# A four-layer vision-mamba stack on one core: the first and the last image's row work moved beside the scans, another order of the scan directions, and empty steps in the side work

## The chip, the cores and the metric

The kernel runs on one NeuronCore of a Trainium2 chip. The metric is the device time of one launch in microseconds. Five engines take part, each with its own instruction queue that is worked off in order: TensorE (PE in the profile, its weight loads PEld), VectorE (DVE), ScalarE (ACT), GpSimd (POOL) and SyncE (SP), which issues all DMAs here. An instruction at the head of a queue that waits for another engine holds up everything behind it in that queue.

## What is computed

Four images of 64 x 64 positions with 128 channels go through four layers. Layers 0, 1 and 3 are selective-scan blocks; layer 2 is a gated block without a scan. The core of a scan block, cut from the reference:

```python
xn = _ln(x); xx, z = split(xn @ in_proj)             # 256 channels each
xc = silu(depthwise_conv3x3(xx) + conv_b)
x0 = xc by rows; x1 = xc by columns                  # L = 4096 positions
xs = stack([x0, x1, x0 reversed, x1 reversed])       # four directions
dts, Bs, Cs = split(x_proj @ xs); delta = softplus(dt_w @ dts + dt_b)
h = exp(delta * A) * h + (delta * x) * B             # 16 states a channel, a scan over L
y = sum over states of h * C, plus Ds * xs; summed over the four directions
y = _ln(y) * silu(z);  x = x + out_proj @ y
x = x + fc2 @ gelu(fc1 @ _ln(x))
```

Layer 2 has two layer norms, products of projections and a mean over the whole image; it sits between the scans of layers 1 and 3.

## The kernel before

**Turns.** One turn is the scan of one image in one scan layer. There are 12 turns, listed in `turns` (L652): images 0 and 1 alternate through layers 0, 1, 3, then images 2 and 3. A turn has 4 directions k (0 and 2 by rows forward and back, 1 and 3 by columns) of 8 chunks each of 512 positions, so 32 chunks. A chunk has 8 periods, a period four `tensor_tensor_scan` on DVE (L799), two with their input from PE (`dbp`, L774) and two with theirs from DVE (`dbv`, L913). ACT makes the decays `da` (L783), POOL multiplies by C (`hc`, L811 and L813), PE sums the states into `yp` (L824), and `leave` (L834) adds `yp` into `y_sb`. Directions run in the order 0, 1, 2, 3. At the end of a turn `leave` issues eight DMAs that store `y_sb` to DRAM (L847).

**Side work.** Everything that is not a scan (output norm, gating, projections, MLP, the gated layer, input norm, convolution) is made by `between(e, frm, to, psums)` (L177) as a list `S` of small steps. It works in rows of 512 positions, 8 rows an image: `output_norm`, `project_z`, `convolve` of the row two back, `silu` with its stores of `x_row` and `x_col`, `mixer_out` (`gate` on POOL, then `project` on PE), `mlp`, then `input_norm`, or `finish` for the last layer, or `gate_sums` and `gate_rest` in the gated layer. With `frm=None` it is the first input norm and convolution of an image (`begin`, `input_norm`, `convolve`). `rest(n)` adds n steps that do nothing, so that other queues may catch up; it stands only after a norm's `mean`, after `project` and after the MLP's `down`, and within `silu`.

While image A is scanned, the steps of image B are dealt out between the scan instructions. `other(number)` (L878) is called four times a period, so a turn has 1024 places ("slots"). It issues steps so that they are spread evenly:

```python
gone = at % (8 * per_turn) * 4 + number
while done < len(steps) and done < len(steps) * (gone - 8) / (4 * 8 * per_turn - 76):
```

that is, over 948 slots from slot 8 on. Turns 1, 2, 7 and 8 carry the plain side work between two scan layers, turns 3, 4, 9 and 10 the gated one, turns 5 and 6 a finished image and a new image's start, turn 11 only a finished image, turn 0 only the start of image 1.

**What no scan covers.** The set-up folds the convolution with the projection for the three scan layers (PE, POOL and DVE, L136 to L154). Then `alone(between(0, None, 0, psums), "first_ps")` runs the start of image 0 with no scan beside it, and after the last scan `alone(after(*turns[-1]), "last_ps")` runs the eight rows of image 3's last layer in the same way. In both, two PSUM banks serve the steps; inside the scans one does.

Of the kernel before, what the change touches and what calls it, by code (L numbers as in the profile page):

```python
# [12 lines left out]
F32 = mybir.dt.float32  # L13
AF = mybir.ActivationFunctionType
ALU = mybir.AluOpType
# [48 lines left out]
def vss_stack_kernel(ctx: ExitStack, tc: tile.TileContext, x: bass.AP, weights, out: bass.AP, n_batch=B, layers=(0, 1, 2, 3)):  # L64
# [25 lines left out]
    wt, conv_d = {}, {}  # L90
    with tc.tile_pool(name="setup", bufs=2) as pool, tc.tile_pool(name="setup_ps", bufs=2, space=PSUM) as psum:
        for i in layers:
            if i == 2:
                g = const.tile([P, GATE_N], F32, name="wg")
                nc.sync.dma_start(out=g, in_=weights[i][0])
                v = {name: g[:, a:z] for name, (a, z) in GATE_AT.items()}

                cb = const.tile([P, 2], F32, name="cb")
                nc.vector.tensor_mul(cb, v["b1"], v["wdw"])
                nc.vector.tensor_add(cb, cb, v["bdw"])  # L100
                v["cb"] = cb
                for name, b, scale in (("b2s", "b2", "beta"), ("bf2s", "bf2", "gamma")):
                    v[name] = const.tile([P, 1], F32, name=name)
                    nc.vector.tensor_mul(v[name], v[b], v[scale])
                wt[i] = v
                continue
            t = const.tile([P, small_n + VSS_N - tail_at], F32, name=f"w{i}")
            for a, z in (VSS_AT["conv_w"], VSS_AT["alog"]):
                nc.sync.dma_start(out=t[:, a - conv_at : z - conv_at], in_=weights[i][0][:, a:z])
            nc.sync.dma_start(out=t[:, small_n:], in_=weights[i][0][:, tail_at:])  # L110
            v = {}
            for name, (a, z) in VSS_AT.items():
                if conv_at <= a < conv_at + small_n:
                    v[name] = t[:, a - conv_at : z - conv_at]
                elif a >= tail_at:
                    v[name] = t[:, small_n + a - tail_at : small_n + z - tail_at]

            v["xp"] = v["xp"].rearrange("p (k m c) -> p k m c", k=2, m=2)
            at, end = VSS_AT["xp"]
            xp = weights[i][0][:, at:end].rearrange("p (b k m c) -> p b k m c", b=2, k=2, m=2)  # L120
            for k in range(2):
                for b in range(2):
                    nc.sync.dma_start(out=v["xp"][:, k, :, b * NX : (b + 1) * NX], in_=xp[:, b, k])
            v["conv_w"] = v["conv_w"].rearrange("p (m t) -> p m t", m=2)
            v["dtb"] = v["dtb"].rearrange("p (k m) -> p k m", k=K)
            a = v["alog"]
            nc.scalar.activation(a, a, AF.Exp)
            nc.vector.tensor_scalar_mul(a, a, -1.0)
            v["a"] = a.rearrange("p (k m n) -> p k m n", k=K, m=2)
            dsum = const.tile([P, 2], F32, name=f"dsum{i}")  # L130
            nc.vector.tensor_reduce(dsum, v["ds"].rearrange("p (k m) -> p m k", k=K), AX.X, ALU.add)
            v["dsum"] = dsum
            v["gelu"] = AF.Gelu if i == 0 else AF.Gelu_apprx_tanh
            wt[i] = v

            in_w = pool.tile([P, DI], F32, tag="in_w", name="in_w")  # L136
            nc.sync.dma_start(out=in_w, in_=weights[i][0][:, :DI])
            conv = pool.tile([P, 2, 9, P], F32, tag="conv", name="conv")
            for m in range(2):
                ps = psum.tile([P, 4, P], F32, tag="ps", name="ps_wt")  # L140
                nc.tensor.transpose(ps[:, 0, :], in_w[:, m * P : (m + 1) * P], ident)
                in_t = pool.tile([P, P], F32, tag="in_t", name="in_t")
                nc.vector.tensor_copy(in_t, ps[:, 0, :])
                diag = pool.tile([P, 9, P], F32, tag="taps", name="taps")
                for t in range(9):
                    nc.gpsimd.tensor_scalar(diag[:, t, :], ident, v["conv_w"][:, m, t : t + 1], None, ALU.mult)
                for t in range(0, 9, 4):
                    count = min(4, 9 - t)
                    ps = psum.tile([P, 4, P], F32, tag="ps", name="ps_taps")
                    for j in range(count):  # L150
                        nc.tensor.matmul(ps[:, j, :], in_t, diag[:, t + j, :], start=True, stop=True)
                    nc.vector.tensor_copy(conv[:, m, t : t + count, :], ps[:, :count, :])
            conv_d[i] = keep.tile([P, 2 * 9 * P], F32, name=f"conv_d{i}")
            nc.sync.dma_start(out=conv_d[i], in_=conv.rearrange("p m t e -> p (m t e)"))  # L154

    def cols(c):
        return slice(c * CH, (c + 1) * CH)


    lanes = []  # L160
    for j in range(2):
# [15 lines left out]
    def between(e, frm, to, psums):  # L177
# [58 lines left out]
        def load():  # L236
# [15 lines left out]
            if frm is None:  # L252
                fetch_x(0)
            else:
                fetch(0)
# [789 lines left out]
```

## Time and profile before

| | us |
|---|---|
| median of 3 runs | 23699.06 (23680.56 to 23713.14) |
| the profiled execution, its time | 23731.97 |
| its span | 23730.2 |
| first scan instruction of turn 0 starts at | 356.50 |
| turns 1, 2, 7, 8 (plain side work), each | 1882 to 1891 |
| turns 3, 4, 9, 10 (gated), each | 2034 to 2048 |
| turns 5, 6 | 1874 and 1876 |
| last scan instruction starts at | 23320.42 |

The profile's page gives each engine's busy time. The answer by windows gives it for any stretch: duration, then each engine's busy time with its number of instructions, the granted TensorE clock, the DMA share and GB/s. The timeline lists instructions in order of time, with the idle time before one in square brackets and the instruction that ended it.

### The profile page before, as it was taken

Reading aid. Unit: us, or ns where it says so; the run is one execution under the profiler, and the core shown is the slowest. Engines: PE = TensorE matmul, PEld = TensorE weight load, DVE = VectorE, ACT = ScalarE, POOL = GpSimd, SP = SyncE. Lnnn points to the kernel's source line nnn. Section 1 sums busy time; section 2 is a strip of 40 time slices with the busy share of each in tenths; the row PEclk is TensorE's granted clock in tenths of the full one; section 3 lists DMA queues with packets and bytes.
Section 4 is the critical chain, followed back from the end, with each engine's and each line's share of the span. In section 5 each row is a group of like instructions: output and inputs, shape, how many; then the busy total and the mean of one; then the engine's idle time right before and its main releaser. Section 6 shows DMA issues by size and latency. Waiting matters only on the chain. (4 is left out here: it accounts for less than half of the span.)

```text
span 23730.2 us, 216913 instructions
## 1 busy us (share of the span) xinstructions
PE 20150.3 (85%) x58234; PEld 10650.4 (45%) x58234; DVE 20432.3 (86%) x20210; ACT 18072.9 (76%) x38792; POOL 19294.9 (81%) x8916
## 2 busy tenths in 40 slices
PE   6888888888888888888888888888888888888886
PEld 3444444444444444444444444444444444444442
DVE  4999998888888888899899889898888888889993
ACT  4777777777877777788788777777777778777774
POOL 4998888888878877788888888888887778788883
PEclk8999999999999999999999999999999999999997
DMA  4444434444334434434434444444443443344331
GB/s 98 139 140 142 131 129 138 130 129 138 124 120 125 136 122 127 132 131 139 137 131 138 133 140 130 127 139 131 130 136 120 121 141 122 120 127 142 129 130 62
DMA packets 2435398, 3060.09 MB, mean 129 GB/s; under 512 B 1753600, under 2 KB 1789056, under 8 KB 2235648
## 3 DMA queue, kind: packets, MB, share of 16 engines
q1 hardware_dynamic: 2434176, 3046.22, 40.8%
q8 instruction: 472, 7.73, 0.1%
q14 instruction: 750, 6.14, 0.1%
HBM read 2784.41 MB, written 261.49 MB: 128 GB/s over the span
## 5 line engine op out<-in xcount | busy, mean ns | idle before, releaser
L811 POOL TENSOR_TENSOR hc<-h,cb 128x1024 f32<-128x1024 f32 x6144 | 14420.8, 2361 | 3596.4 <-DVE h L799 2432.8
L783 ACT ACTIVATE da<-delta,w 128x512 f32<-128x512 f32 x12288 | 8161.9, 713 | 1768.8 <-DVE h L799 1744.1
L824 PE MATMUL yp<-hc,ident 128*128 128x512 f32 x18432 | 9051.9, 617 | 521.6 <-POOL hc L813 310.9
L774 PE MATMUL dbp<-diag,duT 128*128 128x256 f32 x24576 | 6260.7, 400 | 1558.0 <-DVE h L799 1505.2
L799 DVE TENSOR_TENSOR_SCAN h<-da,state,dbp 128x512 f32<-128x512 f32 x5376 | 6563.9, 1261 | 988.7 <-PE dbp L774 807.4
L799 DVE TENSOR_TENSOR_SCAN h<-da,state,dbv 128x512 f32<-128x512 f32 x5376 | 6881.0, 1280 | 487.7 <-ACT da L783 24.1
L774 PEld LDWEIGHTS dbp<-diag,duT 128*128 128x128 f32 x24576 | 4764.8, 199 | 4039.9 <-issue 2586.4
L824 PEld LDWEIGHTS yp<-hc,ident 128*128 128x128 f32 x18432 | 3490.0, 197 | 4862.5 <-issue 3647.9
L913 DVE TENSOR_TENSOR dbv<-dup,bb 128x512 f32<-128x512 f32 x6144 | 4229.9, 688 | 339.4 <-ACT dup L791 175.6
L766 ACT ACTIVATE diag<-ident,bt 128x128 f32<-128x128 f32 x12288 | 3947.9, 401 | 0.3
L813 POOL TENSOR_TENSOR hc<-hc 128x1024 f32<-128x1024 f32 x1536 | 3622.2, 2358 | 120.4
L791 ACT COPY dup<-du 128x512 f32<-128x512 f32 x1920 | 1126.3, 587 | 1336.9 <-DVE dbv L913 1309.8
L361 PE MATMUL gap<-halo,cw 128*128 128x512 f32 x3456 | 1703.8, 606 | 3.1 <-ACT wide L368 3.1
L734 POOL TENSOR_TENSOR du<-delta,xs 128x512 f32<-128x512 f32 x768 | 978.7, 1274 | 114.0 <-ACT delta L722 114.0
L799 DVE TENSOR_TENSOR_SCAN h<-da,dbp 128x512 f32<-128x512 f32 x768 | 893.4, 1201 | 163.4 <-PE dbp L774 104.4
L717 PE MATMUL ps_dt<-xd,dt_w 8*128 8x512 f32 x1536 | 894.0, 662 | 150.1 <-ACT delta L720 85.8
L799 DVE TENSOR_TENSOR_SCAN h<-da,dbv 128x512 f32<-128x512 f32 x768 | 937.4, 1221 | 69.2 <-DVE dbv L913 3.3
L807 ACT COPY state<-h 128x2 f32<-128x2 f32 x5376 | 960.7, 179 | 0.0
L361 PEld LDWEIGHTS gap<-halo,cw 128*128 128x128 f32 x3456 | 639.8, 193 | 698.8 <-issue 666.6
L742 ACT COPY duT<-ps_duT 128x512 f32<-128x512 f32 x768 | 440.1, 573 | 285.5 <-PE ps_duT L740 285.1
L443 PE MATMUL gap<-hid,pw 128*128 128x512 f32 x768 | 455.5, 710 | 166.1 <-ACT hid L434 165.1
L720 ACT ACTIVATE delta<-ps_dt,w 128x512 f32<-128x512 f32 x768 | 524.2, 683 | 46.1 <-PE ps_dt L717 41.4
(122 smaller groups left out, 11353.9 us busy)
## 6 DMA issues: line engine op xcount, KB each, us to landing
cb<-xd_d SPq DMA_DIRECT2D x1536, 1024.0 KB
bb<-xd_d SPq DMA_DIRECT2D x1536, 512.0 KB
xs<-x_row_d SPq DMA_DIRECT2D x192, 512.0 KB
xs<-x_col_d SPq DMA_DIRECT2D x192, 512.0 KB
x_col_d<-down SPq DMA_DIRECT2D x192, 256.0 KB
x_row_d<-wide SPq DMA_DIRECT2D x96, 512.0 KB
y_d<-y_sb SPq DMA_DIRECT2D x96, 512.0 KB
y<-y_d SPq DMA_DIRECT2D x96, 512.0 KB
```

Source lines behind the costliest of these rows:

```text
L361: nc.tensor.matmul(z.ps, z.cw[:, m, t, :], z.halo[c][:, dy : dy + RPC, dx : dx + W], start=(t == 0), stop=(t == 8))
L734: nc.gpsimd.tensor_mul(s.du[:, m], s.delta[:, m], s.xs[:, m])
L766: nc.scalar.activation(s.diag[q][:, t, :, j], ident, AF.Copy, scale=s.bt[:, t, CQ * q + j : CQ * q + j + 1])
L774: nc.tensor.matmul(s.db[:, t * P : (t + 1) * P, :], s.duT[:, t, m, :], s.diag[q][:, t], start=True, stop=True)
L783: nc.scalar.activation(da[:, j], s.delta[:, m], AF.Exp, scale=s.v["a"][:, s.k, m, n : n + 1])
L791: nc.scalar.copy(s.dup, s.du[:, m])
L799: nc.vector.tensor_tensor_scan(s.h[i, side][:, j, s.step], da[:, j, s.step], db[:, s.step], init, ALU.mult, ALU.add)
L807: nc.scalar.copy(s.state[:, m, n : n + 2].unsqueeze(2), s.h[i, side][:, :, s.end : s.end + 1])
L811: nc.gpsimd.tensor_mul(hc, s.h[i, side], s.cb[i // 2][:, 2 * side : 2 * side + 2, :])
L813: nc.gpsimd.tensor_add(hc, hc, s.hc[i, 0])
L824: nc.tensor.matmul(getattr(s, f"yp{m}"), ident, s.hc[i, side][:, j], start=opens and j == 0, stop=i == end and side == 1 and j == 1,)
L913: nc.vector.tensor_mul(db, s.dup, s.bb[i // 2][:, j])
```

## The change

1. **Set-up.** The folding of the convolution weights becomes a list of steps, `combine(i, psums)`, which uses ACT and PE and works four taps at a time. `combine(0)` runs before the first scan, `combine(1)` and `combine(3)` among the side work of turn 0.
2. **First image.** `between` returns its steps row by row. Of image 0's start (`opening`) only rows 0 to 3 run before the first scan; rows 4 to 9 run in turn 0's chunks 0 to 5, one a chunk. The rest of turn 0's side work is spread from slot 190 to slot 956.
3. **Last image.** In the last turn image 2's last rows are spread over slots 8 to 808. Image 3's rows then follow one a chunk: the row with index n takes the slots from n x 32 + 8 to (n + 1) x 32 + 8, n from 25 on, in descending order of position (`order`). What is left after the last scan is run there.
4. **Order of directions.** 0, 1, 3, 2 in the first turn and 1, 3, 0, 2 in the others. The first one (`nth == 0`) writes `y_sb` with the `Ds` term, through a column view where it goes by columns. In the last direction each chunk of `y_sb` is stored as soon as it is complete.
5. **Empty steps.** `rest` is added in the norms (`output_norm` has the same ones but the last), around `gate`, after `gelu` and after additions, and at both places of `gate_rest` where `plus` adds on POOL; `breath` is 1 in plain work and 0 in the gated one. In the gated work a convolution step issues three taps rather than one.

```diff
+    def combine(i, psums):
...
+        def turn(m):
+            z.ps = psums[0].tile([P, CH], F32, tag="gap", name="gap")
+            nc.tensor.transpose(z.ps[:, :P], z.in_w[:, m * P : (m + 1) * P], ident)
...
+        def taps(m, t, count):
+            z.taps = gap1.tile([P, 4, P], F32, tag="t", name="taps")
+            for j in range(count):
+                nc.scalar.activation(z.taps[:, j], ident, AF.Copy, scale=wt[i]["conv_w"][:, m, t + j : t + j + 1])
...
+        def leave(m, t, count):
+            conv = gap1.tile([P, 4 * P], F32, tag="y", name="conv")
+            nc.scalar.copy(conv[:, : count * P], z.ps[:, : count * P])
+            at = (m * 9 + t) * P
+            nc.sync.dma_start(out=conv_d[i][:, at : at + count * P], in_=conv[:, : count * P])
...
     def between(e, frm, to, psums):
...
-        pause, delayed = (2 if gated else 3), []
+        order = list(range(NCH)) if to is not None else list(range(NCH))[::-1]
+        pause, breath, delayed = (2 if gated else 3), (0 if gated else 1), []
...
@@ norm, output_norm @@
-            S.extend((centre, square, variance, root, scale, affine))
+            S.extend((centre, square))
+            rest(1)
+            S.extend((variance, root))
+            rest(breath)
+            S.append(scale)
+            rest(breath)
+            S.append(affine)
+            rest(1)
...
         def output_norm(c):
+            if to is None:
+                S.append(lambda: fetch(c))
+                rest(2)
...
         def convolve(c):
+            stride = 3 if gated else 1
...
@@ mixer_out @@
-            S.extend((gate, project, lambda: fetch(c + 1)))
+            rest(1)
+            S.append(gate)
+            rest(1 + breath)
+            S.append(project)
+            if to is not None:
+                S.append(lambda: fetch(c + 1))
             rest()
             S.append(add)
+            rest(1)
...
@@ mlp @@
             S.append(gelu)
+            rest(1 + breath)
...
@@ gate_rest @@
             S.extend((project, lambda: scaled(g["b2s"], g["beta"]), plus))
+            rest(2)
...
-        for k in range(K):
+        for nth, k in enumerate((1, 3, 0, 2) if turn else (0, 1, 3, 2)):
...
     def meanwhile(turn):
+        chunk, end = 4 * 8, 4 * 8 * (per_turn - 2) - 4
+        if not turn:
+            first = [(row, n * chunk, (n + 1) * chunk - 2) for n, row in enumerate(opening[4:])]
+            rest = combine(1, psums), combine(3, psums), *between(turns[1][0], None, 0, psums)
+            return first + spaced(rest, first[-1][2], end)
+        rows = after(*turns[turn - 1])
+        if turn + 1 == len(turns):
+            last = [(row, n * chunk + 8, (n + 1) * chunk + 8) for n, row in enumerate(after(*turns[turn]), 3 * NCH + 1)]
+            return spaced(rows, 8, last[0][1]) + last
+        if turns[turn + 1][1] == 0:
+            rows += between(turns[turn + 1][0], None, 0, psums)
+        return spaced(rows, 8, end)
...
@@ leave @@
+            if s.nth == 0:
+                nc.vector.scalar_tensor_tensor(y, xs, s.v["dsum"][:, m : m + 1], yp, ALU.mult, ALU.add)
             else:
-                nc.vector.tensor_add(y_sb[:, m, cols(s.c)], y_sb[:, m, cols(s.c)], yp)
-            if s.k == K - 1 and s.last and m == s.flip:
-                for c in range(NCH):
-                    nc.sync.dma_start(out=lanes[s.e % 2].y[:, :, cols(c)], in_=y_sb[:, :, cols(c)])
+                nc.vector.tensor_add(y, y, yp)
+            if s.nth == K - 1 and m == s.flip:
+                nc.sync.dma_start(out=lanes[s.e % 2].y[:, :, cols(s.c)], in_=y_sb[:, :, cols(s.c)])
...
+        for step in sum([combine(0, psums)] + opening[:4], []):
+            step()
         s = chunks[0]
...
@@ other @@
-                while done < len(steps) and done < len(steps) * (gone - 8) / (4 * 8 * per_turn - 76):
-                    steps[done]()
-                    done += 1
+                for todo, count, frm, to in segments:
+                    while todo and count - len(todo) < count * (gone - frm) / (to - frm):
+                        todo.pop(0)()
...
-    alone(between(0, None, 0, psums), "first_ps")
-    alone(after(*turns[-1]), "last_ps")
```

## The prediction

> **What bounds the kernel now.** I read the windows by stage first. Columns: stretch, duration, busy time of PE, PEld, DVE, ACT and POOL, granted clock, DMA share, GB/s.
>
> ```profile
> 0.00:356.00 356.00, 203.61 (x494) 94.57 (x494) 23.84 (x54) 97.07 (x137) 35.81 (x80) 0.75 0.45 61
> 356.00:2064.00 1708.00, 1479.59 (x4502) 793.66 (x4501) 1644.74 (x1615) 1356.18 (x3041) 1569.09 (x721) 0.98 0.46 141
> 2064.00:3955.00 1891.00, 1643.73 (x4768) 874.68 (x4768) 1690.03 (x1664) 1469.78 (x3179) 1595.29 (x730) 0.95 0.41 132
> 5846.00:7880.00 2034.00, 1716.69 (x4930) 904.47 (x4930) 1725.17 (x1717) 1550.29 (x3306) 1625.87 (x756) 0.95 0.41 127
> 9928.00:11802.00 1874.00, 1633.72 (x4832) 872.47 (x4832) 1690.43 (x1665) 1491.98 (x3215) 1595.00 (x731) 0.96 0.43 136
> 21533.00:23322.00 1789.00, 1507.03 (x4454) 804.78 (x4455) 1675.94 (x1648) 1403.93 (x3080) 1591.53 (x711) 0.96 0.37 132
> 23322.00:23730.00 408.00, 223.01 (x331) 79.58 (x329) 44.57 (x50) 151.09 (x176) 21.56 (x10) 0.71 0.11 36
> ```
>
> The reader is to see three things. Two stretches without scans last 356 and 408 us with DVE nearly idle. In the turns between, DVE is the bound: in turn 0 it is idle for 1708 - 1645 = 63 us, which I take as the floor. Above that floor, DVE's idle time is 138 us in a plain turn (1), 246 in a gated one (3), 121 in turn 5 and 50 in turn 11: the side work's stalls. Then I read the groups of instructions over the twelve turns for what PE waits for (last part: idle before, by releaser):
>
> ```profile
> L443 PE MATMUL gap<-hid,pw 128*128 128x512 f32 x704 | 406.0, 689 | 134.1 <-ACT hid L434 133.1
> L204 PE MATMUL gap<-res,mean 128*128 128x512 f32 x480 | 284.2, 676 | 187.8 <-POOL res L580 179.7 <-DVE res L408 3.3 <-ACT res L290 2.8
> L405 PE MATMUL gap<-y,pw 128*128 128x512 f32 x352 | 242.0, 825 | 197.2 <-POOL y L400 197.1
> L305 PE MATMUL gap<-y,mean 128*128 128x512 f32 x352 | 188.8, 663 | 154.9 <-DMA y<-y_d 154.9
> ```
>
> and the timeline, for how such a wait reaches the scans:
>
> ```profile
> 5483.52 3.37 PE L405 MATMUL gap<-y,pw 128*128 128x512 f32 x4 [8.85 <-POOL y L400]
> 5488.76 2.45 DVE L799 TENSOR_TENSOR_SCAN h<-da,state,dbp 128x512 f32<-128x512 f32 x2 [8.59 <-PE dbp L774]
> ...
> 4357.78 2.45 DVE L799 TENSOR_TENSOR_SCAN h<-da,state,dbp 128x512 f32<-128x512 f32 x2 [2.41 <-PE dbp L774]
> ```
>
> `project` waits 8.85 us for `gate`, the scan's matmuls stand behind it, and the scan starts 8.59 us late. In the third line no PE wait precedes: convolution taps (L361) fill PE. Last, the two bare stretches in the timeline and, for the final two lines, in the chain:
>
> ```profile
> 45.36 1.08 PE L286 MATMUL gap<-ident,xt 128*128 128x128 f32 x4 [10.77 <-DMA xt<-in_x]
> 61.85 17.68 PE L361 MATMUL gap<-halo,cw 128*128 128x512 f32 x36
> 92.59 0.69 DVE L208 TENSOR_TENSOR cen<-res,gap 128x512 f32<-128x512 f32 x1 [28.51 <-DMA x_col_d<-down]
> 102.38 16.20 PE L361 MATMUL gap<-halo,cw 128*128 128x512 f32 x36
> 335.23 1.94 PE L710 MATMUL ps_x<-xs,w 128*80 128x512 f32 x4 [0.78 <-ACT wide L368]
> 356.50 2.33 DVE L799 TENSOR_TENSOR_SCAN h<-da,dbp 128x512 f32<-128x512 f32 x2 [52.42 <-ACT da L783]
> ...
> 23344.11 3.75 PE L305 MATMUL gap<-y,mean 128*128 128x512 f32 x4 [16.37 <-DMA y<-y_d]
> ...
> 23396.17 3.64 PE gap L317 x4
> 23443.93 3.65 PE gap L317 x4
> ```
>
> A first row costs 102.38 - 61.85 = 40.5 us alone (the `x_col` store holds `cen`), a last row 47.8.
>
> **Opening: -193.** Row 0 starts at 45.4 once the set-up is done. Now the loads of all layers go first (some 12 us of issue) and `combine(0)` follows: six batches of about 4 us at most (four 0.4 us ACT copies, up to 1.5 us of matmul, a 0.6 us copy, in series), again about 45; I count nothing, +-8. One PSUM bank in place of two costs these serial rows the 0.7 us of a `take`, nothing more. Rows 2 and 3 (convolutions 0 and 1) end at 61.9 + 2 x 40.5 = 143; from the prologue's first matmul to the first scan it is 21 us (335.2 to 356.5), partly behind row 3's last steps: first scan at 163 instead of 356.
>
> **Turn 0: +85.** PE's spare time prices convolution. A row's 18 taps are 36 PE passes of 0.43 us, 15.5 us. PE's slack beside a scan is about 2.0 us a period of 6.7 (1.5 by busy time, which is modelled long; 2.0 makes a plain turn's 26 slots, 6.5 periods, 2.5 us short, as the 2.41 us line has it). Rows 4 to 7 put 20 steps in 12.5 slots, 3.1 periods: 15.5 - 6.2 = 9.3 each; rows 8 and 9 in 5.4 periods: 4.8 each. Sum 47. The rows' other stages at 1.6 steps a slot: some 6 us each, 24. In it are their DMAs, six a row, which now stand in SP's queue before the scans' `bb` and `cb` loads: alone, an `x_row` store took 4.53 us to issue behind an `x_col` store; a `cb` load is issued about a period, 6.7 us, ahead, so this is hidden unless two of them meet. Both ends of the 24: 0, and 60 if every row waits for both its `x_col` stores, 7.5 us each. DVE's own work 5; two `combine` lists (36 ACT copies beside an idle ACT, PE some 7 us) 9. Image 1's start, spread over 766 slots, still fits: its taps take 9 periods, slack 18.
>
> **Turns 1 to 10: -316.** I counted the list lengths. Plain: 723 steps become 867 in the same 948 slots, so a step takes 1.09 slots, not 1.31. From `gate` to `project` it was 1.31 slots and is 3.28 (6 us), likewise `gelu` to `down`; `root` to `scale` becomes 2.19. Turn 11 before (441 steps, 2.15 slots a step) shows what such spacing leaves: 50 - 12 for its first wait = 38, 4.8 us a row. I take 6. Against it, taps are denser: 22 slots, 5.5 periods, 4.5 us short. And the start of a turn: the first `mean` waits 154.9/11 = 14 us for `y`, behind eight stores that take 8.9 us to issue on SP; now one store, about 1.3, precedes, so the wait and its knock-on of about 16 falls to 8. Plain: 8 x (6 + 4.5) + 8 = 92 against 138, -46, four times. Turns 5 and 6 (793 to 953 steps; taps in 5 periods, 5.5 short): 8 x 11.5 + 7 = 99 against 121, -22, twice. Gated (1021 to 1069): `plus` to `mean` and `gate` to `project` gain about a slot or two, so from (246 - 16 - 8 x 6.2)/8 = 22.5 us a row to 15; but three taps a step put a row's 15.5 us into 7.1 slots, 1.8 periods: 12 short. 8 x 27 + 8 = 224, -22, four times. Sum 184 + 44 + 88 = 316.
>
> **Turn 11: +164.** Image 2's rows at 0.71 steps a slot: 45 against 50. Image 3's rows: 71 steps in 32 slots, 2.2 a slot, so all rests shrink below half. ACT carries the scans' 39.7 us a chunk (turn 0's 1356 less eight rows of 10.8, over 32) and a last row's 20: 59.7 against 53.4 a chunk, so at least 6 us; the upper bound is the row alone, 47.8. The nearest row is the gated turn's 22.5 at half this density, in about twice the stages; I take 25. In it is a wait of some 5 us for `y`: a chunk's `y` is stored and loaded again at once (the load alone 6 us, in the tail 23338.0 to 23344.1), while `mean` follows `fetch` by three steps, 2.7 us; PE stands, and `dbp` behind it. Slots cover 6.75 rows: 169. Here a rule speaks against the change: the Trainium skill, "ScalarE: Activation LUTs", section "What ACT_TABLE_LOAD costs", puts a drain of about 1.38 us behind each load of 1.28. A last row has four. In this trace the activation follows its load at once (load 23715.46 to 23716.74, gelu at 23716.75), so I count 1.28; with the drains ACT would reach 65 and the seven rows cost up to 37 more.
>
> **Ending: -342.** The last scan ends at 23321.7 (23320.42 + 1.28), 408.5 us before the span does. What stays: the wait for `yp`, one store and `y`, 16 us (22.4 before, with eight stores), and one row, 47.8; the quarter of row 6 that is left runs under that wait. 66, -342.
>
> **Order of directions: -10.** An addition through columns takes 1.27 us (L842), by rows 0.66, the first write 0.72 by rows. Through columns the latter isn't in the trace; between 0.72 and twice the column addition, 1.27 by nearness: 16 x (1.27 + 1.27) + 32 x 0.66 = 61.8 against 62.7 a turn; ends -110 and +220 over eleven turns, neither likely. Storing a chunk at once adds no DMA, and SP waits for a `leave` that DVE is just doing.
>
> **Sum.** -193 + 85 - 316 + 164 - 342 - 10 = -612. The profiled execution took 23732, 0.14% above the median 23699; scaled to the median, 23699 - 611 = 23088.
>
> **The rivals.** (a) *Rests remove nearly all stalls*: for, turn 11's 4.8 a row; against, the taps. With 3 us of taps a row (7 in gated turns) and 6 for the first wait: plain 8 x 7.8 + 6 = 68, turns 5 and 6 71, gated 8 x (10 + 7) + 6 = 142: -280 - 100 - 416 = -796 for the ten turns, 22609. (b) *Rests give nothing*: gains at `gate` and `gelu` come back as tap shortage, as the same work is denser elsewhere; for, `take`s stay one step behind their matmuls; ten turns at 0, 23404. (c) *Dense rows are as dear as alone*, since one long chain runs through all queues: 6.75 x 47.8 = 323, 23242; against, nothing in a gated turn costs half of that. (d) *Slower: bursts of taps.* In a gated row six bursts of three taps (2.6 us each) stand before `dbp`; if each delays a whole period's chain of ACT, POOL and DVE, 6.7 us, the row loses 40, not 12: 28 x 32 = 896, 23984. It decides from 12 + 611/32 = 31 us a row. Against it: 15.5 us is all the PE time there is to lose. (e) *The bare stretches don't shrink*, since turn 0 must wait for rows: row c is needed only in chunk c - 1 and made in chunk c - 2, so I give it no number.
>
> **How the numbers follow.** Chances: main 0.58 (its own range 22850 to 23300), a 0.17, b 0.11, c 0.09, d 0.05. Range 22680 to 23360, which leaves out half of (a), a part of (b) and (d). About 0.2%, 47 us, is what this measurement can tell from no change. Faster 0.94, within 0.2% 0.01, slower 0.05.
>
> **What would show it.** First scan near 163; 66 us after the last scan; turn 0 near 1793, plain turns near 1845, gated near 2012, turn 11 near 1950 with chunks of 78 at its end; L405's and L443's waits gone in plain turns, L305's halved. Gated turns above 2040 speak for (d), chunks near 100 at the end for (c). Plain turns still at 1890 would sink the step on rests.

## The result and the profile after

The changed kernel takes 23326.36 us (median, 23323.90 to 23332.58) against 23699.26 on the same chip: ratio 0.9844, 95% interval 0.9826 to 0.9861, 373 us less. The forecast was 23088 with a range of 22680 to 23360. The direction is right and the time lies in the range, but the gain is 0.61 of the 611 expected, and the time lies above the main forecast's own range (22850 to 23300) and nearer to rival (b)'s 23404 than to 23088. The profiled execution took 23325.13 us with a span of 23323.4.

The windows of the changed kernel, by stage (stretch, duration, busy time of PE, PEld, DVE, ACT and POOL, granted clock, DMA share, GB/s): what precedes the first scan, turns 0, 1, 3 and 5, turn 11 cut where its dense rows begin, and what follows the last scan:

```profile
0.00:165.60 165.60, 80.93 (x170) 35.91 (x170) 7.09 (x23) 50.35 (x95) 3.87 (x19) 0.81 0.42 82
165.60:1999.30 1833.70, 1611.32 (x4824) 871.97 (x4824) 1656.01 (x1623) 1422.71 (x3161) 1571.77 (x728) 0.96 0.47 138
1999.30:3852.80 1853.50, 1618.02 (x4768) 859.20 (x4768) 1684.86 (x1666) 1467.32 (x3182) 1594.35 (x731) 0.97 0.43 135
5713.20:7744.30 2031.10, 1726.70 (x4930) 908.63 (x4930) 1717.96 (x1717) 1550.39 (x3305) 1625.06 (x755) 0.95 0.41 127
9771.30:11659.50 1888.20, 1646.03 (x4832) 876.37 (x4832) 1687.47 (x1665) 1490.82 (x3216) 1595.49 (x732) 0.96 0.44 135
21329.00:22667.00 1338.00, 1151.69 (x3433) 616.18 (x3433) 1264.65 (x1248) 1089.05 (x2366) 1199.22 (x537) 0.97 0.38 134
22667.00:23244.70 577.70, 472.65 (x1284) 237.32 (x1283) 441.60 (x444) 432.82 (x863) 410.68 (x182) 0.93 0.33 115
23244.70:23323.40 78.70, 44.01 (x69) 14.09 (x67) 7.41 (x10) 26.89 (x30) 4.69 (x2) 0.72 0.09 27
```

DVE still bounds the turns: its busy time has hardly moved, and what changed is its idle time (duration less DVE's busy time: turn 1 from 201 us to 169, turn 3 from 309 to 313, turn 5 from 184 to 201). All stages, as time after less time before, beside the forecast:

| stage | change, us | forecast |
|---|---|---|
| up to the first scan (356.5 to 165.6) | -191 | -193 |
| turn 0 (1707.4 to 1833.7) | +126 | +85 |
| turns 1, 2, 7, 8 (plain) | -136 | -184 |
| turns 3, 4, 9, 10 (gated) | -35 | -88 |
| turns 5, 6 | +32 | -44 |
| turn 11 (1788.8 to 1915.7) | +127 | +164 |
| after the last scan (408.5 to 78.7) | -330 | -342 |
| sum | -407 | -602, and -10 for the order |

The sum is -407 and not -373 since the profiled execution of the kernel before took 33 us more than its median (23732 against 23699). Of the 195 us that are missing, 177 lie in the ten middle turns (-139 where -316 was forecast; 48 in plain turns, 76 in turns 5 and 6, 53 in gated ones); what turn 0 and the ending lack, 41 and 12, is largely made up by turn 11, which is luck. The groups of instructions of the changed kernel over the scans say why. The last part of a line is the idle time before the group and who ended it:

```profile
L984 DVE TENSOR_TENSOR dbv<-dup,bb 128x512 f32<-128x512 f32 x6144 | 4226.0, 688 | 614.2 <-ACT dup L862 400.7 <-DMA bb<-xd_d 112.8 <-ACT state L878 2.2
L495 PE MATMUL gap<-hid,pw 128*128 128x512 f32 x752 | 394.0, 640 | 85.9 <-ACT hid L485 85.9
L226 PE MATMUL gap<-res,mean 128*128 128x512 f32 x502 | 274.4, 629 | 55.2 <-POOL res L633 48.8 <-ACT res L319 6.4
L450 PE MATMUL gap<-y,pw 128*128 128x512 f32 x380 | 214.0, 692 | 45.8 <-POOL y L445 45.5
L338 PE MATMUL gap<-y,mean 128*128 128x512 f32 x380 | 202.2, 659 | 55.1 <-DMA y<-y_d 51.7 <-ACT delta L791 3.4
L245 DVE TENSOR_TENSOR cen<-cen,gap 128x512 f32<-128x512 f32 x251 | 169.8, 676 | 228.6 <-ACT gap L242 228.5
L413 ACT ACTIVATE wide<-gap,w 128x512 f32<-128x512 f32 x188 | 129.4, 688 | 789.1 <-PE gap L402 789.0
```

The four waits of PE that the prediction named have shrunk: for `gate` from 197 to 46 us, for `gelu` from 133 to 86, for the addition on POOL from 180 to 49, for `y` from 155 to 52. But two waits have grown that its sum did not price. ACT stands before the `take` of a convolution. In the kernel before, the same group read:

```profile
L368 ACT ACTIVATE wide<-gap,w 128x512 f32<-128x512 f32 x176 | 120.7, 686 | 431.2 <-PE gap L361 431.1
```

and DVE's `dbv` waits 401 us for `dup`, a copy in ACT's queue, where it waited 176 (and 113 us for the load of `bb`, where it waited 62). ACT is not the bound, but `delta`, `da` and `dup` of the scans stand behind whatever ACT waits for. One `take` of this kind in the timeline, and one late `dup` with the 5.11 us that DVE loses for it:

```profile
2415.27 0.69 ACT L413 ACTIVATE wide<-gap,w 128x512 f32<-128x512 f32 x1 [3.81 <-PE gap L402]
...
2852.14 1.28 ACT L421 ACT_TABLE_LOAD   x1
2853.44 1.91 ACT L421 ACTIVATE wide<-wide 128x2048 f32<-128x2048 f32 x1
2855.36 1.28 ACT L220 ACT_TABLE_LOAD   x1
2856.66 0.59 ACT L862 COPY dup<-du 128x512 f32<-128x512 f32 x1
2857.28 0.70 DVE L984 TENSOR_TENSOR dbv<-dup,bb 128x512 f32<-128x512 f32 x1 [5.11 <-ACT dup L862]
```

### The profile page after: what moved, and what is told of

Read it like the earlier page. It is cut to its first block, busy times and chain, and to the rows that moved or that the text cites. A ratio compares the mean times of both kernels' runs of the same rounds, so it can differ in the third digit from the quotient of the medians.

```text
span 23323.4 us, 216855 instructions
## 1 busy us (share of the span) xinstructions
PE 20052.7 (86%) x58234; PEld 10604.8 (45%) x58234; DVE 20362.5 (87%) x20186; ACT 18075.1 (77%) x38870; POOL 19260.3 (83%) x8862
## 5 line engine op out<-in xcount | busy, mean ns | idle before, releaser
L413 ACT ACTIVATE wide<-gap,w 128x512 f32<-128x512 f32 x192 | 132.1, 688 | 824.2 <-PE gap L402 824.1
```

## The experiments

The leading theory after the result: the empty steps do take away the waits for which they were put in, but the same list of steps then stands denser elsewhere, and the taps of the convolution with a `take` one step behind them cost what the prediction left out. The rival: the empty steps bring little, and the gain is that of the ends alone. The diffs are against the changed kernel unless said otherwise. Turns that an edit does not touch differ by up to 15 us between kernels (turns 3 and 5 of experiment 4 by +14 and -15), so a single turn is read no finer than that. The kernel before took 23690 to 23696 us beside the experiments and 23699 beside the changed kernel, so totals are compared with the changed kernel to within some 10 us.

**1. Without the added empty steps.** All added `rest`s out but the two behind `fetch` in the last layer, and one tap a step in gated turns.

```diff
-            S.extend((centre, square))
-            rest(1)
-            S.extend((variance, root))
-            rest(breath)
-            S.append(scale)
-            rest(breath)
-            S.append(affine)
-            rest(1)
+            S.extend((centre, square, variance, root, scale, affine))
...
-            stride = 3 if gated else 1
+            stride = 1
```

> The changed kernel without part 5: no added empty steps, one tap a step in the gated work; parts 1 to 4 stay. The changed kernel's turns are: plain 1851 to 1860, gated 2027 to 2037, turns 5 and 6 1888 and 1893, turn 11 1916, 23323 in all. Theory A (the empty steps take stalls away in plain turns, but pack the taps): without them plain turns rise by 20 to 30 each, turns 5 and 6, whose lists shrink from 953 to about 800 steps, fall by 20 to 35 each, gated turns change by less than 10, turn 11 falls by 0 to 15 as its dense rows have fewer steps to issue; total 23330 to 23400. Theory B (the empty steps do nothing, and the turns differ from before by the first wait for y and by the order of directions alone): every turn within 6 of the changed kernel's, total 23300 to 23350. As predicted (rests are worth 30 a plain turn, 22 less of taps in the gated ones): total about 23450.

Measured: 23436.66 us, ratio to the kernel before 0.9894 (0.9865 to 0.9923), 110 us over the changed kernel. Plain turns are 13 to 22 us longer, gated ones 3 to 18; turns 5 and 6 are 5 and 13 us shorter, and turn 11 is 21.5 longer, where a fall was expected. The groups show the waits back:

```profile
L964 DVE TENSOR_TENSOR dbv<-dup,bb 128x512 f32<-128x512 f32 x6144 | 4227.9, 688 | 393.5 <-ACT dup L842 238.7 <-DMA bb<-xd_d 54.1 <-ACT diag L817 0.8
L478 PE MATMUL gap<-hid,pw 128*128 128x512 f32 x768 | 450.8, 702 | 167.3 <-ACT hid L469 166.8
L226 PE MATMUL gap<-res,mean 128*128 128x512 f32 x512 | 309.6, 690 | 221.3 <-POOL res L615 189.9 <-ACT res L312 22.6 <-DVE res L440 8.4
L437 PE MATMUL gap<-y,pw 128*128 128x512 f32 x384 | 275.2, 856 | 248.3 <-POOL y L432 248.3
```

So the empty steps are worth some 110 us, together with the bursts of three taps, which this edit takes out as well; 95 us of it lie in the ten middle turns. They take about 410 us of PE's waits away (167 + 190 + 248 here against 94 + 49 + 51 over the whole changed kernel), and the late `dup`s that come with them (239 to 401) are part of what they give back. They pay in turn 11 as well.

**2. One order of directions in all turns.**

```diff
-        for nth, k in enumerate((1, 3, 0, 2) if turn else (0, 1, 3, 2)):
+        for nth, k in enumerate((0, 1, 3, 2)):
```

> The changed kernel with the directions in the order 0, 1, 3, 2 in every turn rather than 1, 3, 0, 2 from the second one on. Theory A (the order by itself costs and gains nothing; what grew in turns 5 and 6 and in the waits for dup comes from the lists of steps): every turn within 6 of the changed kernel's, total 23300 to 23345. Theory B (starting with the columns moves the convolution rows beside other chunks and makes the waits for dup, 400 in all against 176 before): turns 5 and 6 fall by 20 or more each, waits for dup fall below 250, total 23150 to 23280.

Measured: 23290.88 us, ratio 0.9832 (0.9804 to 0.9861), 35 us below the changed kernel, with overlapping intervals. Turns 5 and 6 are 15 and 21 us shorter, plain turns 1 to 11 longer. The wait for `dup` stays at 397: the order is not its cause.

**3. One tap a step in the gated turns.**

```diff
-            stride = 3 if gated else 1
+            stride = 1
```

> The changed kernel with one tap a step in the gated turns too; their lists grow from 1069 to 1165 steps. Theory A (a burst of three taps makes PE late by what it lacks, 12 us a row, where single taps over 16 slots lack 7): the four gated turns fall by 15 to 35 each, total 23180 to 23265. Theory B (PE's total is what counts, and bursts free slots for the rests): gated turns rise by 0 to 25 each, total 23325 to 23420.

Measured: 23269.71 us, ratio 0.9823 (0.9795 to 0.9852). The four gated turns change by 0, -9, -13 and -7 (a fall of 15 to 35 each was expected by the one theory, a rise by the other), and the untouched turns together by -28 as well. Of the 57 us, then, about half at most belong to the taps, and a burst of three taps costs little against three single ones. Experiment 8 repeats this on a better kernel.

**4. The ends bare again.** The opening's ten rows before the first scan, image 3's rows after the last one, everything else as changed.

```diff
-            first = [(row, n * chunk, (n + 1) * chunk - 2) for n, row in enumerate(opening[4:])]
+            first = [([], 0, 190)]
...
-            return spaced(rows, 8, last[0][1]) + last
+            return spaced(rows, 8, end) + [(row, 1 << 20, (1 << 20) + 32) for row, *_ in last]
...
-        for step in sum([combine(0, psums)] + opening[:4], []):
+        for step in sum([combine(0, psums)] + opening, []):
```

> Parts 2 and 3 undone: all ten rows of image 0's start run before the first scan, and image 3's last eight rows after the last scan; the order of directions, the empty steps and the folding of weights stay as changed. Theory A (the ledger by stages: 191 us of opening and 330 of ending bought with 126 in turn 0 and 127 in turn 11): first scan at about 365, turn 0 at 1710 to 1725, turn 11 at 1780 to 1795, 400 to 420 after the last scan, total 23580 to 23640. Theory B (turn 0 and turn 11 grew for another reason, such as the order of directions or the folding in turn 0): they stay above 1800 and 1850, and the total exceeds 23700.

Measured: 23649.74 us, ratio 0.9982 (0.9975 to 0.9990). Its windows (first stretch, turn 0, turn 11, what follows the last scan):

```profile
0.00:408.30 408.30, 207.66 (x418) 86.33 (x418) 12.60 (x30) 106.47 (x164) 4.50 (x26) 0.76 0.41 56
408.30:2123.00 1714.70, 1493.37 (x4576) 807.58 (x4576) 1646.93 (x1615) 1371.91 (x3092) 1570.10 (x721) 0.98 0.45 142
21432.10:23189.20 1757.10, 1492.96 (x4454) 797.05 (x4455) 1670.37 (x1649) 1402.70 (x3081) 1591.78 (x712) 0.97 0.37 134
23189.20:23645.30 456.10, 248.30 (x331) 75.28 (x329) 43.43 (x50) 152.15 (x176) 21.85 (x10) 0.63 0.08 26
```

The moved rows cost turn 0 1833.7 - 1714.7 = 119 us and turn 11 1915.7 - 1757.1 = 159, and the two ends together are worth 323 us. Turn 0 with the folding but without the rows is 7 us over the kernel before (1707.4). Both bare stretches are longer than before (408 against 356, 456 against 408), which was not expected. In the opening some 20 of the 52 us are a wait of the scan's first projection for its `xs` load (20.99 us; before, it waited 0.78 us in all). For the rest, a row alone became dearer. The timeline of PE shows where. First the kernel before, in a bare row, from the MLP's first product to its last and on to the next row; then the changed kernel's last row:

```profile
23421.86 6.14 PE L426 MATMUL gap<-t,pw 128*128 128x512 f32 x8 [2.93 <-ACT t L230]
23432.00 6.19 PE L443 MATMUL gap<-hid,pw 128*128 128x512 f32 x8 [4.00 <-ACT hid L434]
23439.04 0.66 PE L496 MATMUL gap<-ident,res 128*128 128x128 f32 x4 [0.84 <-DVE res L448]
23439.53 1.88 PE L305 MATMUL gap<-y,mean 128*128 128x512 f32 x4
```

```profile
23264.37 0.65 PE L549 MATMUL gap<-ident,res 128*128 128x128 f32 x4 [0.84 <-DVE res L500]
23265.70 1.98 PE L338 MATMUL gap<-y,mean 128*128 128x512 f32 x4 [0.68 <-ACT ot L553]
...
23297.53 2.07 PE L477 MATMUL gap<-t,pw 128*128 128x512 f32 x2 [2.93 <-ACT t L252]
23300.44 2.08 PE L477 MATMUL gap<-t,pw 128*128 128x512 f32 x2 [0.84 <-ACT hid L480]
...
23312.22 5.79 PE L495 MATMUL gap<-hid,pw 128*128 128x512 f32 x8 [4.00 <-ACT hid L485]
```

With two PSUM banks the four products run through without a wait, 10.1 us to the next stage. With one, each waits for the `take` of the one before: 14.7 us. The waits themselves are 0.84 + 0.78 + 0.78 = 2.4 of these 4.5 us. The rest is the products: PE is busy 8.3 us with them in place of 6.1, at a lower granted clock (the number before the last two). The windows of this stretch, before and after:

```profile
23421.86:23432.00 10.14, 6.14 (x8) 2.28 (x9) 0.00 (x0) 5.98 (x7) 0.00 (x0) 0.67 0.08 26
23297.53:23312.22 14.69, 8.30 (x8) 2.00 (x9) 0.00 (x0) 5.98 (x7) 0.00 (x0) 0.50 0.00 0
```

The clock was 0.50 where it had been 0.67, and over the whole bare stretch 0.63 where it had been 0.71. It fell together with the waits; whether they are its cause, no run here separates. The next row's `mean` also waits for the copy of the finished row out of the bank (`ot`, 1.33 us behind the transposes rather than 0.49). That is 4.5 + 0.8 = 5.4 of the 6.8 us by which such a row is dearer (54.6 on average here, (23640.8 - 23258.9) / 7, against 47.8).

**5. The eight stores of `y` at the turn's end again** (turns 0 to 10).

```diff
-            if s.nth == K - 1 and m == s.flip:
-                nc.sync.dma_start(out=lanes[s.e % 2].y[:, :, cols(s.c)], in_=y_sb[:, :, cols(s.c)])
+            if s.nth == K - 1 and m == s.flip and (s.last or s.turn + 1 == len(turns)):
+                for c in range(NCH) if s.turn + 1 < len(turns) else (s.c,):
+                    nc.sync.dma_start(out=lanes[s.e % 2].y[:, :, cols(c)], in_=y_sb[:, :, cols(c)])
```

> The changed kernel, but in turns 0 to 10 all eight chunks of y_sb are stored at the end of the turn, as before; the last turn still stores chunk by chunk. Theory A (the first row of a turn waits less because one store rather than eight stands before its load on SP): the first chunks of turns 1 to 11 go back from 53 to 67 us to 66 to 76, 118 us in all over ten turns and 12 in turn 11, total 23420 to 23470. Theory B (the first chunks are shorter because of the order of directions and the empty steps before the first use): first chunks within 3 of the changed kernel's, total 23300 to 23345.

Measured: 23404.56 us, ratio 0.9877 (0.9848 to 0.9906), 78 us more than the changed kernel. The first chunks of turns 1 to 11 are together 104 us longer, and the wait for `y` is back at the 155 of the kernel before:

```profile
L338 PE MATMUL gap<-y,mean 128*128 128x512 f32 x384 | 208.0, 669 | 154.2 <-DMA y<-y_d 153.6 <-ACT ot L553 0.7
```

So storing each chunk at once is worth 78 us in all (85 in the windows of turns 1 to 10, where the prediction took 8 a turn, 80), and the 118 + 12 written down for this run were too much.

With these five the account closes roughly: from the kernel before to experiment 4's, -110 (empty steps and bursts) - 78 (stores) + 35 (order) + 52 + 48 (longer bare stretches) = -53, measured -50 (-41 against the kernel before of the same session); and the ends' -323 more give the -373 of the change. It can't be read finer than some 25 us, since 28 of the 110 lie in turns 0 and 11, where experiment 4 has no rows.

**6. A later `take`.** Two empty steps between a convolution's last tap and its `take`.

```diff
                     S.append(taps)
...
+                rest(2)
                 S.append(take)
```

> The changed kernel with two empty steps between the last tap of a convolution and the take on ACT that reads it (four more steps a row). Theory A (with denser taps PE is behind, the take stands at the head of ACT's queue until PE has caught up, 789 us in all against 431 before, and dup and the decays behind it come late): waits of that take fall below 350, DVE's waits for dup from 406 to under 280, plain turns and turns 5 and 6 fall by 8 to 20 each, gated ones by 10 to 30, total 23090 to 23230. Theory B (PE lacks the time itself, so DVE waits for dbp instead of dup): waits for dup fall, waits for dbp rise by as much, total 23300 to 23345.

Measured: 23241.22 us, ratio 0.9808 (0.9780 to 0.9836), 85 us below the changed kernel. Plain turns are 12 to 27 us shorter, turns 5 and 6 28 and 36; the gated ones are 9 to 17 longer, where a fall was expected. Turn 1 in the groups, first of the changed kernel, then of this one:

```profile
L870 DVE TENSOR_TENSOR_SCAN h<-da,state,dbp 128x512 f32<-128x512 f32 x448 | 546.6, 1259 | 56.7 <-PE dbp L845 50.2 <-ACT diag L837 3.0 <-ACT da L854 2.5
L413 ACT ACTIVATE wide<-gap,w 128x512 f32<-128x512 f32 x16 | 11.0, 689 | 42.6 <-PE gap L402 42.6
...
L871 DVE TENSOR_TENSOR_SCAN h<-da,state,dbp 128x512 f32<-128x512 f32 x448 | 546.6, 1260 | 48.1 <-PE dbp L846 41.3 <-ACT da L855 4.6 <-ACT state L879 1.5
L413 ACT ACTIVATE wide<-gap,w 128x512 f32<-128x512 f32 x16 | 10.9, 680 | 4.7 <-PE gap L402 4.7
```

ACT's wait before the `take` falls from 789 us to 328 over the scans: in plain turns and turns 5 and 6 from 305 to 42, in the gated ones from 410 to 226. In the six turns that became shorter (145 us together) DVE waits less for `dbp` (374 to 318 us) and for `bb` (76 to 28), but little less for `dup` (174 to 159). Over all turns the wait for `dup` is 422 us and does not fall: that half of the theory is refuted.

**7. Several steps set later together.** The order of 2, the late `take` of 6, one empty step from `root` to `scale` in gated norms too, and three in place of one between the POOL product and its sum on DVE.

```diff
             S.extend((variance, root))
-            rest(breath)
+            rest(1)
...
             S.extend((first, take, second, last, product))
-            rest(1)
+            rest(3)
```

> The changed kernel with the order 0, 1, 3, 2 in every turn, two empty steps before a convolution's take, one more empty step between root and scale in the gated turns' norms, and three rather than one between product and total there. Theory A (each wait for a partner one step away is DVE's own loss: 228 us of scale on root and 79 of total on product): turns 5 and 6 fall by 25 to 40 each, gated ones by 35 to 70, plain by 5 to 20, total 22980 to 23150. Theory B (denser lists give it back elsewhere): gated turns within 10 of the changed kernel's, total 23230 to 23300.

Measured: 23076.15 us, ratio 0.9738 (0.9710 to 0.9767), 250 us below the changed kernel. The gated turns are now at 1993 to 2002, 32 to 44 below the changed kernel, though the late `take` alone had made them longer.

**8. The same with one tap a step.** 

> As e7_combined, with one tap a step in the gated turns as well; their lists grow from 1149 to 1245 steps in the 948 slots. Theory A (bursts make PE late): gated turns fall by 5 to 30 more each than in e7_combined. Theory B (over 1.3 steps a slot the added empty steps shrink to nothing): they rise by 5 to 30 each.

Measured: 23081.87 us, ratio 0.9741 (0.9712 to 0.9769): 6 us from experiment 7, gated turns 1995 to 1999. Over a turn, three taps in a burst cost what three single taps cost. Within it they don't quite: the first chunk of a gated turn is 8 to 11 us longer here, and the rest of the turn as much shorter.

**9. Experiment 7 with the late `take` in plain work only** (`rest(0 if gated else 2)`; this run and the next on another chip, where the kernel before took 23690 us). 

> As e7_combined, but the two empty steps before a convolution's take stand only where the work is not gated; the gated lists shrink from 1149 to 1117 steps. Theory A (in the gated turns these steps cost 14 a turn, as e6_late_take had it, since they pack everything else): the gated turns fall by 5 to 20 each from 1997, the others stay, total 23000 to 23060. Theory B (in e6_late_take the gated turns rose for want of the step between root and scale, which is there now): gated turns within 5, total 23065 to 23090.

Measured: 23279.49 us, ratio 0.9827 (0.9813 to 0.9842); the gated turns are at 2043 to 2051, 44 to 58 us above experiment 7. Both theories missed this. One gated turn in the groups, first of experiment 7, then of this one:

```profile
L871 DVE TENSOR_TENSOR_SCAN h<-da,state,dbp 128x512 f32<-128x512 f32 x448 | 547.5, 1261 | 94.8 <-PE dbp L846 76.0 <-POOL du L806 10.9 <-ACT da L855 5.0
L985 DVE TENSOR_TENSOR dbv<-dup,bb 128x512 f32<-128x512 f32 x512 | 352.7, 689 | 54.1 <-ACT dup L863 31.6 <-DMA bb<-xd_d 14.7
L413 ACT ACTIVATE wide<-gap,w 128x512 f32<-128x512 f32 x16 | 11.0, 687 | 52.6 <-PE gap L402 49.2 <-issue 3.3
```

```profile
L871 DVE TENSOR_TENSOR_SCAN h<-da,state,dbp 128x512 f32<-128x512 f32 x448 | 548.0, 1261 | 107.3 <-PE dbp L846 97.8 <-ACT da L855 7.3 <-ACT diag L838 1.6
L985 DVE TENSOR_TENSOR dbv<-dup,bb 128x512 f32<-128x512 f32 x512 | 352.7, 689 | 68.5 <-ACT dup L863 51.2 <-DMA bb<-xd_d 9.3
L413 ACT ACTIVATE wide<-gap,w 128x512 f32<-128x512 f32 x16 | 11.0, 687 | 105.8 <-PE gap L402 105.8
```

ACT waits 106 us before the `take` in place of 49, and the scans wait longer for `dbp` (98 against 76) and `dup` (51 against 32). The late `take` is worth 50 us a gated turn here and cost some 14 in experiment 6: the places of the steps don't add up one by one.

**10. Experiment 9, and the gated work's other steps later:** `scale` a step behind `root` in the output norm, two steps behind `gelu` and before `project`.

```diff
-            rest(1 + breath)
+            rest(2)
```

> As e9_take_plain_only, and in the gated turns one more empty step between root and scale of the output norm, after gelu and between gate and project, so that these distances are the plain turns' in steps; the lists grow to 1141. Theory A (DVE's remaining waits for root in the output norm, 15 a turn, and PE's for gelu, 15, and gate, 9, fall): gated turns fall by 10 to 25 each more. Theory B (the lists are full, and each added step takes from another distance): within 5 or up by 10.

Measured: 23169.34 us, ratio 0.9781 (0.9765 to 0.9798); gated turns 2013 to 2021, 24 to 36 us less than in experiment 9 (10 to 25 expected).

**11. Experiments 7 and 10 together.** 

> e7_combined with the three further empty steps of e10_gated_more in the gated turns: all empty steps tried so far together, order 0, 1, 3, 2, three taps a step in gated turns; gated lists 1173 steps. Theory A (the gains add: the late take 48 a gated turn beside e9, the further steps 30 beside e9): gated turns near 1970, total 22940 to 23000. Theory B (the lists are full at 1.24 steps a slot): gated turns within 12 of e7_combined's 1997, total 23030 to 23120.

Measured: 23014.38 us, ratio 0.9712 (0.9698 to 0.9725); gated turns 1978 to 1981, 47 to 58 below the changed kernel; the total lies between the two expectations. DVE's two waits for a partner one step away, over the whole kernel:

```profile
L245 DVE TENSOR_TENSOR cen<-cen,gap 128x512 f32<-128x512 f32 x256 | 172.8, 675 | 160.3 <-ACT gap L242 160.1
L593 DVE TENSOR_REDUCE sums<-g 128x1 f32<-128x512 f32 x32 | 21.3, 666 | 8.4 <-POOL g L590 8.4
```

In the changed kernel they are 262 us (`scale` on `root`) and 79 us (`total` on `product`): 172 us less, where the four gated turns lose 212.

**12. One more step between `variance` and `root` in gated norms.**

```diff
-            S.extend((variance, root))
-            rest(breath)
+            S.append(variance)
+            rest(1 - breath)
+            S.append(root)
+            rest(1)
```

> e11_all_late with one empty step between variance and root in the gated turns' norms; lists grow by 40 to 1213 steps. Theory A (ACT still waits about 40 a gated turn at the head of its queue for the variance, and dup stands behind it): gated turns fall by 5 to 20 each. Theory B (the added steps pack the rest): they rise by 0 to 15 each.

Measured: 22997.22 us, ratio 0.9706 (0.9693 to 0.9720); gated turns 1980 to 1982, the same as in experiment 11, so this step changes nothing. It is the fastest kernel here, though not distinguishable from experiment 11's: 329 us below the changed kernel and 702 below the one before.

## Why the prediction was right in direction and too large in size

**Ends: right, two terms off.** The opening's -191 is the -193 foretold, by errors that cancel: row 0 began at 40.5 us rather than 45.4, convolutions 0 and 1 stand 44.7 us apart rather than 40.5, and the prologue begins at 146.8 rather than 143 but takes 18.8 rather than 21. The timeline of the changed kernel:

```profile
40.47 1.09 PE L315 MATMUL gap<-ident,xt 128*128 128x128 f32 x4 [9.08 <-DMA xt<-in_x]
59.42 10.67 PE L402 MATMUL gap<-halo,cw 128*128 128x512 f32 x18 [2.13 <-issue]
104.10 10.52 PE L402 MATMUL gap<-halo,cw 128*128 128x512 f32 x18 [2.18 <-DVE cen L245]
146.75 3.64 PE L781 MATMUL ps_x<-xs,w 128*80 128x512 f32 x4 [0.29 <-DMA xs<-x_row_d]
165.58 2.33 DVE L870 TENSOR_TENSOR_SCAN h<-da,dbp 128x512 f32<-128x512 f32 x2 [17.08 <-ACT da L854]
```

The convolution is now two groups of 18 passes with a `take` between, where it was one of 36. The failed step is "one PSUM bank in place of two costs these serial rows the 0.7 us of a `take`, nothing more": it costs a last row 5.4 us. After the last scan 78.7 us remain, not 66: the wait for `y` is 21.0 (23244.7 to 23265.7), not 16, and the row takes 57.7, not 47.8. Of these 9.9 us, 3.9 are a slip: 47.8 is the distance of two rows, while the last row of the kernel before takes 51.7 to the end of the span (23678.5 to 23730.2). Nor does the prediction's sum come out: 16 + 47.8 is 63.8 and not 66.

**Turn 0: +126, not +85.** Without the rows turn 0 is only 7 us dearer than before (9 foretold for the folding). The rows cost 119 where 47 + 24 + 5 = 76 was forecast; with the upper end of 60 for their stages it would be 112. The trace of the first six chunks (421.1 us against 313.4 in experiment 4) suggests that both terms were too small. DVE waits 59 us for `dbp`, where 47 stood for the taps, and 21 for `dup`, 10 for `bb` and 5 for `da`, where 24 stood for the stages; in experiment 4 the waits for `dbp`, `dup` and `bb` come to under 3 us there. A wait for `dbp` can have another cause than the taps, though, and no run separates the two.

**Turn 11: +127, not +164.** The rows' 159 us against 169 confirm the 25 us for a dense row, the chunks with them taking 71 to 77 us (78 foretold). The miss is in image 2's rows: experiment 4's turn 11 has 1757.1 - 1670.4 = 87 us of DVE idle time, 24 above the floor of 63, where 45 was left of 50. Of the 26 us that went, 13 lie in the first chunk (65.6 to 52.5 us). Rival (c), rows as dear as alone, is out.

**Plain turns and turns 5 and 6: the failing step.** The prediction let a row's stages keep 6 us of stall. It priced the taps by PE's missing time (4.5 and 5.5 us a row) and counted nothing for the `take` behind them. With 1.09 slots a step (turns 5 and 6: 953 steps in 948 slots) in place of 1.31, that `take`, one step behind its last tap, reaches ACT before PE is done, and ACT stands: 305 us in these six turns in place of 182. Two more steps in front of it (experiment 6) take that to 42 us and bring plain turns to 1830 to 1839 (1845 forecast) and turns 5 and 6 to 1857 and 1860 (1852 forecast). Rival (b) had named this `take`, and the result lies on its side of the forecast, though short of it: the empty steps do bring 110 us. The ten turns by terms: of the -316, 80 stood for the first wait, where experiment 5 measures 85, and 236 for empty steps and bursts, where experiment 1 measures 95. The order of directions, counted apart, cost 31 us there (experiment 2). (The three come to 149, the windows to 139.) So the wait for `y` was sized rightly, and the net gain of the empty steps was put at more than twice what it is.

**Gated turns: a term that wasn't there.** The forecast took 12 us a row for three taps in a burst and a gain from 22.5 to 15 for the other stages. Experiment 8 finds no cost in bursts against single taps over a turn, so rival (d), 40 us a row, falls. Rivals (a) and (e) are out as well: the ten turns gained 139 us and not 796, and both bare stretches shrank. Yet the gated turns gained only 9 us each, what the first chunk alone gave: the empty steps left the rest of the row's stalls where they were, since `scale` followed `root` at once, the `take` its taps, and `down` the `gelu` and `total` the `product` with one step between. Later places for them bring each gated turn 47 to 58 us (experiment 11; its order of directions alone brought 6 a turn in experiment 2). Most of this is DVE's own waits for `root` and for `product`, which fall by 172 us in all. The stalls lay in those distances and not in the bursts.

**Order of directions.** `leave` takes less than forecast, 59.3 us a turn (61.8 foretold, 62.7 before), since a first write through columns costs 1.09 us and not 1.27 (the 192 first writes take 204.0 us; sixteen of them, in turn 0, go by rows at 0.72).

Against one order for all turns (experiment 2) this is worth nothing; that one is rather 35 us faster, though the intervals overlap.

**The rule that spoke against it.** The drain of about 1.38 us that the Trainium skill ("ScalarE: Activation LUTs", section "What ACT_TABLE_LOAD costs") adds to a table load is not seen here either: in the timeline above, the load of 2852.14 lasts 1.28 us and the `silu` behind it starts at 2853.44. The dense rows stayed below a forecast that was made without it.

**What stays open.** DVE's wait for `dup` rose from 176 us to 401, and the runs tell two parts of it. In turns 0 and 11 it rose from 7 us to 96 with the rows moved there (12 in experiment 4, which leaves them out). In the ten middle turns it rose from 169 to 305 with the empty steps (171 in experiment 1, which leaves those out); a later `take` (422 in all), the other order (397) and single taps (409 in experiment 3) don't lower it. In these 305 us ACT is idle for 2: it works through `da`, `down`, `silu`, `gelu` and table loads that stand before `dup` in its queue. Why the empty steps set more of that work before `dup` is open. Why the gated turns' distances don't add up is not settled either; where in a scan's period a step falls shifts with every length of the list, and no run holds that fixed.

## What to carry to other kernels

When side work is dealt out between the instructions of a bound engine, an empty step helps at the place where an engine would stand, and it makes all other distances in the same list shorter: price every producer and consumer that stay one step apart, those on engines with time to spare included, since the bound engine's helpers queue behind them. Moving work from bare stretches beside a bound engine saved about half of its time here: 620 us left the bare stretches (864 in experiment 4 to 244), and 278 were added to turns 0 and 11. A resource cut to one, here the PSUM bank, must be priced in every serial chain that used two.

## What the runs showed that was not expected

Two empty steps before a `take` made gated turns 9 to 17 us longer in one kernel and 50 us shorter in another that differed in a few distances of the same list. Turns whose instructions and order were not touched moved by up to 15 us between two kernels, so that a step worth less than that in one turn can't be told from one trace of it. And with one PSUM bank in place of two, the MLP's first products in a bare row took 2.2 us longer themselves, at a granted clock of 0.50 in place of 0.67, beside the 2.4 us of their waits.
